# A four-layer graph network on one core: an addition moved one step in VectorE's order, and the first transposes of each attended pair laid apart

## The chip, the cores and the metric

The kernel runs on one core of a Trainium2 chip, in one launch. The metric is the time of one execution on the device in microseconds (us), as the median of several runs. A profile is one execution with every instruction recorded; its page and its views give times from the start of the span. The engines are named as the profile names them: PE is TensorE (matmuls and transposes), PEld its weight loads, DVE is VectorE, ACT is ScalarE, POOL is GpSimd, SP is the queue that issues the DMAs.

## The reference, cut to what matters

`x` has 3327 rows (nodes) of 256 numbers, `adj` is a 3327 x 3327 matrix, and all is fp32. Four layers follow one another, each `x = layernorm(x + layer(x, adj))`. The change lies in the fourth:

```python
def _top_p_attention(X, W1, W2, W3):
    logits = (X @ W1.T @ W2.T) @ (X @ W3.T).T
    probs = softmax(logits)
    ...                       # keep, in each row, the largest up to a sum of 0.9
    A = probs * mask
    return A / A.sum(-1)

R = (S + I) / rowsum          # S is adj
for n in range(2):
    A = _top_p_attention(Xa, W1, W2, W3)
    Xf = R @ Xf               # "diffusion"
    Xa = A @ Xa               # "attention"
    Z = Z + Xf @ U1[n].T + Xa @ U2[n].T
h = X + Z
```

The change touches the first of these two rounds only (n = 0), the "first attention".

## The kernel before, in words

The 3327 rows are padded to 26 tiles of 128 rows (`nt` = 26, `nh` = 13). In the first attention the tiles are worked in pairs, 13 of them. Each pair takes three kinds of work:

- Diffusion (`diffused_pair`, from L1219): R @ X for two row tiles at once, in 13 steps ("columns"). The seven products of a column are the seven of Strassen's scheme for a 2 x 2 block product (`products`, L1166); their operands are sums that VectorE makes (`cb`) from tiles that are loaded two columns at a time (`part`, L1221: three DMAs into `at`, three buffers).
- Attention (`attended_pair`, from L1250): the same seven products with the masked exponentials `es` of the pair. Here every column must first be transposed. `turn(j)` makes four transposes into one PSUM tile named `tp` and ScalarE copies it to `wt`; `mix()` makes the sums `sw` from `wt` in three VectorE instructions. Three columns are turned and two mixed ahead of the first product; from there each step turns column j + 3, mixes column j + 2 and multiplies column j.
- The two row tiles of the pair before are finished in `first` (from L1550), a generator of steps. It scales the attention's result on ScalarE, transposes it together with the diffused tile (`xt`, a VectorE copy out of a `tp` tile), multiplies by U1[0] and U2[0] into one half of a second `tp` tile, `ps`, and by U1[1] into its other half. VectorE adds X to the first half (`s`, stored in DRAM as `sd` over SP), ScalarE copies the second half into `Y`, which is the name of `F` in the profile. Another step makes the products with U2[1] (`pg`, a third `tp` tile) and the keys and queries of the second attention.

For a tile's exponentials there is a search for the top-p threshold, `search_short` (from L1388), a generator as well. Nearly all of it is VectorE's: 26 MAX8 over segments (`cand`), six rounds of MAX8 and MATCH_REPLACE (`top`, `rest`), a sum over the ranks (`lim`, `cs`, `over`, `v`), and two passes over the two halves of the tile `e`, each 1664 columns wide, that zero what falls below the threshold. ScalarE does the exponentials. A tile can be transposed only when the pass over its second half is done.

The order is written out by hand. During this part of the program PE and VectorE run strictly in the order in which the generators are stepped (the flag `fixed` and the class `Fixed`, L873 to L885). ScalarE, GpSimd and SP instructions are put in order by the framework's scheduler, which also makes every wait. The loop over the pairs (from L1739) interleaves the steps. For pair i it first runs a "stage" of seven steps, k = 0 to 6 (`stage`, L1692). Each step k gives

1. one column of the diffusion of pair i + 1 (`spread`),
2. what `then` holds for k: at k = 0 `end_pair` closes the attention of pair i - 1; at k = 5 `attend_to` finishes all open searches (`finish`), and takes the first step of pair i's attention,
3. on even k one group of logits of the next tile (four matmuls into `sc`, ScalarE copies them to `e`),
4. on k = 2, 3, 4 one step of `first`,
5. some steps of the running search (`looks`).

Seven attention columns follow, then a second stage of six steps with the rest of the diffusion, another tile's logits and `first` of the other tile of the pair before, and the last six attention columns. The pool `psum` gives `tp` two buffers, so that every new `tp` tile waits until the tile but one before has been read. The buffer `s` has one copy, which `first` uses twice: for the sum with X and later for the products with U2[1].

The lines that matter below: L1263 (ACT's copy `wt` in `turn`), L1404 and L1408 (ACT's exponentials in the search), L1160 and L1163 (ACT's copies of the logits), L1553, L1570 and L1577 (ACT in `first`), L1569 (the DMA of `s`), L1329 (ACT's copy in the last two tiles' attention, which are done one at a time). PE and VectorE instructions of this part all carry L891, the line of the helper that records the order.

Of the kernel before, what the change touches and what calls it, by code (L numbers as in the profile page):

```python
# [50 lines left out]
def gnn_kernel(ctx: ExitStack, tc: tile.TileContext, n: int, a: dict, out: bass.AP):  # L51
    nc = tc.nc
# [124 lines left out]
    with tc.tile_pool(name="l1b", bufs=1) as wpool, tc.tile_pool(name="l1at", bufs=2) as l1at:  # L177
# [3 lines left out]
        with tc.tile_pool(name="l0", bufs=1) as pool, tc.tile_pool(name="l0w", bufs=2) as work, \  # L181
# [30 lines left out]
            for i in range(nh):  # L212
# [12 lines left out]
                for r in range(2):  # L225
                    it = 2 * i + r
# [13 lines left out]
        with tc.tile_pool(name="l1aw", bufs=1) as cwork, tc.tile_pool(name="l1c", bufs=2) as ch, \  # L240
# [499 lines left out]
            turned = []  # L740
            for k, (c, s) in enumerate(states):
# [61 lines left out]
                if c and 9 <= s < 9 + tiles_of(c - 1):  # L803
                    rs, nb = plus[:2]
                    i = s - 9
# [44 lines left out]
            for i in range(m):  # L850
                it = starts[nch - 1] // P + i
# [16 lines left out]
    with tc.tile_pool(name="l3", bufs=1) as pool, tc.tile_pool(name="l3d", bufs=1, space=DRAM) as dram:  # L868
# [26 lines left out]
        def project_keys(ps, it, xt):  # L895

            h = it * P // half
            for k in range(2):
                tensor.matmul(ps, wkq[h][:, k, :], xt[:, k, :], start=(k == 0), stop=(k == 1))

        def store_keys(work, ps, p, it):

            h, j = divmod(it * P, half)
            key, query = (slice(x * DA, (x + 1) * DA) for x in (h, 1 - h))
            nc.scalar.copy(kT[p][key, j:j + P], ps[key, :])
            q = work.tile([2 * DA, P], F32, name="q")
            nc.scalar.copy(q[query, :], ps[query, :])
            for x in (0, DA):
                nc.sync.dma_start(qd[p][it, x:x + DA, :], q[query, :])
# [94 lines left out]
        with tc.tile_pool(name="l2c", bufs=1) as cpool:  # L1004
# [5 lines left out]
            with tc.tile_pool(name="l2a", bufs=1) as wpool, \  # L1010
# [36 lines left out]
                ps = psum.tile([1, 1], F32, name="ps")  # L1047
# [84 lines left out]
        Y = F[:, :, :D]  # L1132
# [33 lines left out]
        def products(pa, y, w, b):  # L1166

            own, mix = pa[:, 0, :], pa[:, 1, :]
            a11, a12, s1, a22, s2, s3, s4 = w
            b11, b21, b22, t1, t2, t3, t4 = b  # L1170
            for k, (acc, x, v) in enumerate(((own[:, :HD], a11, b11), (own[:, HD:D], a12, b21), (own[:, D:D + HD], s1, t1),
                                             (mix[:, :HD], s4, b22), (mix[:, HD:D], a22, t4),
                                             (mix[:, D:D + HD], s2, t2), (mix[:, D + HD:], s3, t3))):
                tensor.matmul(acc, x, v[:, y, :], start=(y == 0 and k in (0, 3)), stop=(y == nh - 1 and k in (2, 6)))

        def assembled(work, pa):

            p1, p2, p5, p3, p4, p6, p7 = (pa[:, k // 3, k % 3 * HD:(k % 3 + 1) * HD] if k < 6 else pa[:, 1, 3 * HD:] for k in range(7))
            c = work.tile([P, 2, D], F32, name="c", bufs=1)
            v, u = c[:, 0, HD:], c[:, 1, HD:]  # L1180
            vector.tensor_copy(v, p1)
            vector.tensor_add(c[:, 0, :HD], p2, v)
            vector.tensor_sub(v, p6, v)
            vector.tensor_sub(u, v, p7)
            vector.tensor_add(v, v, p5)
            vector.tensor_sub(v, p3, v)
            vector.tensor_sub(c[:, 1, :HD], u, p4)
            vector.tensor_add(u, u, p5)
            return c
# [62 lines left out]
        def attended_pair(quads, psum, es, b):  # L1252

            pa = psum.tile([P, 2, 512], F32, name="acc")
            wts, ws = [], []

            def turn(j):
                pt = psum.tile([P, 4, P], F32, name="tp")
                for r, e in enumerate(es):
                    for h in range(2):  # L1260
                        tensor.transpose(pt[:, 2 * r + h, :], e[:, (h * nh + j) * P:(h * nh + j + 1) * P], ident)
                wts.append(quads.tile([P, 4, P], F32, name="wt", bufs=4))
                nc.scalar.copy(wts[-1], pt)  # L1263

            def mix():
                wt = wts.pop(0)
                sw = quads.tile([P, 4, P], F32, name="sw", bufs=3)
                vector.tensor_tensor(sw[:, :2, :], wt[:, ::3, :], wt[:, 2:3, :].to_broadcast([P, 2, P]), op=ALU.add)
                vector.tensor_add(sw[:, 2, :], sw[:, 1, :], wt[:, 0, :])
                vector.tensor_add(sw[:, 3, :], sw[:, 2, :], wt[:, 1, :])  # L1270
                a11, a12, a21, a22, s3, s1, s2, s4 = (x[:, k, :] for x in (wt, sw) for k in range(4))
                ws.append((a11, a12, s1, a22, s2, s3, s4))

            for j in range(3):
                turn(j)
            for j in range(2):
                mix()
            yield None
            for j in range(nh):
                if j + 3 < nh:  # L1280
                    turn(j + 3)
                if wts:
                    mix()
                products(pa, j, ws.pop(0), b)
                yield None
            yield assembled(quads, pa)
# [263 lines left out]
        def first(work, psum, it, acc, f, xf, tag="pj", xa=None):  # L1550

            xa = work.tile([P, D], F32, name="h") if xa is None else xa
            nc.scalar.mul(xa, acc, f)  # L1553
            yield
            pt = psum.tile([P, 4, P], F32, name=tag)
            for i, v in enumerate((xf, xa)):
                for k in range(2):
                    tensor.transpose(pt[:, 2 * i + k, :], v[:, k * P:(k + 1) * P], ident)
            xt = work.tile([P, 4, P], F32, name="xt", bufs=1)
            vector.tensor_copy(xt, pt)  # L1560
            yield
            ps = psum.tile([P, 4, P], F32, name=tag).rearrange("p (k x) d -> p k (x d)", k=2)
            for k in range(4):
                tensor.matmul(ps[:, 0, :], xt[:, k, :], (u1 if k < 2 else u2)[:, 0, k % 2, :], start=(k == 0), stop=(k == 3))
            for k in range(2):
                tensor.matmul(ps[:, 1, :], xt[:, k, :], u1[:, 1, k, :], start=(k == 0), stop=(k == 1))
            s = work.tile([P, D], F32, name="s")
            vector.tensor_add(s, ps[:, 0, :], X[:, it, :])
            nc.sync.dma_start(sd[it], s)  # L1569
            nc.scalar.copy(Y[:, it, :], ps[:, 1, :])  # L1570
            yield
            pg = psum.tile([P, 4, P], F32, name=tag).rearrange("p (k x) d -> p k (x d)", k=2)
            for k in range(2):
                tensor.matmul(pg[:, 0, :], xt[:, 2 + k, :], u2[:, 1, k, :], start=(k == 0), stop=(k == 1))
            project_keys(pg[:, 1, :P], it, xt[:, 2:, :])
            g = G[:, it, :] if tag == "pj" else work.tile([P, D], F32, name="s")
            nc.scalar.copy(g, pg[:, 0, :])  # L1577
            if tag != "pj":
                nc.sync.dma_start(gd[it], g)
            store_keys(work, pg[:, 1, :P], 1, it)  # L1580
            yield
# [70 lines left out]
        with tc.tile_pool(name="l3w", bufs=2) as work, tc.tile_pool(name="l3s", bufs=4) as sm:  # L1652
# [13 lines left out]
            with tc.tile_pool(name="l3p", bufs=2, space=PSUM) as psum, tc.tile_pool(name="l3a", bufs=1) as quads:  # L1666
# [39 lines left out]
                def attend_to(i):  # L1706
                    turned[0] = attended_pair(quads, psum, (es[2 * i], es[2 * i + 1]), b)
                    finish()
                    next(turned[0])

                turned = [None]
                none = [iter(())]
                todo = [none, none]

                def end_pair(i):
                    c = next(turned[0])
                    for r in range(2):
                        it = 2 * i + r
                        f = normalizer(sm, kepts[0][:, it:it + 1], tots[0][:, it:it + 1])
                        todo[r] = [first(quads, psum, it, c[:, r, :], f, xfs[it], "tp", c[:, r, :])]  # L1720
                        next(todo[r][0])
                    ends[0] = todo[0][0]
# [15 lines left out]
                ends = [iter(())]  # L1738
                for i in range(nh - 1):  # L1739
                    stage(spread, 7, logits(2 * i + 2), ends, counts,  # L1740
                          {0: lambda: end_pair(i - 1) if i else None, 5: lambda: attend_to(i)})
                    counts = [1, 2, 2, 2, 2, 0, 0]
                    queue.append(searches[2 * i + 2])
                    values = turned[0]
                    for k in range(7):
                        next(values)
                        looks(k in (1, 2, 4, 5, 6))
                    stage(spread, 6, logits(2 * i + 3), todo[1], [2, 1, 2, 1, 2, 1], {})
                    finish()
                    queue.append(searches[2 * i + 3])  # L1750
                    for k in range(6):
                        next(values)
                        if k == 0:
                            for _ in spread:
                                pass
                        if k == 3:
                            spread = spreading(i + 2)
                        looks(k > 1)
# [245 lines left out]
```

## Time and profile before

| | us |
|---|---|
| median of 3 runs (3407.56, 3408.01, 3412.42) | 3408.01 |
| the profiled execution | 3412.8 |
| its span, first to last instruction | 3411.0 |
| PE busy in the span | 3129.6 (92%) |
| DVE busy | 2687.8 (79%) |
| ACT busy | 1729.9 (51%) |
| POOL busy | 1132.1 (33%) |

The profiled execution is 4.8 us above the median; 1.8 us of it lie outside the span. The first attention with its attended pairs lies between about 1755 and 2570 us of the span. Its 12 pairs of the loop repeat every 65.30 us: the fourth transpose of an attended pair starts at 1820.10, 1950.71, 2016.01, 2342.52 and 2473.13, for example, which are multiples of 65.30 apart. Busy time of PE is summed from modelled ends, and matmuls are pipelined; so the distance between the starts of two instructions is the surer measure of what a stretch takes. "[1.06 <-DVE e L891]" after an entry of the timeline means that the engine stood idle for 1.06 us before it and that a VectorE instruction on the tile `e` ended that wait. A count such as x5 joins five instructions of one kind into one entry, which begins with the first of them.

### The profile page before, as it was taken

The numbers are of one execution on the slowest core, as the hardware profiler recorded it, in microseconds if no ns is written. First come the engines' busy times: TensorE is split into PE (matmuls) and PEld (weight loads), VectorE is DVE, ScalarE is ACT, GpSimd is POOL, SyncE is SP. The second block draws the span as 40 slices with busy tenths as digits, with TensorE's granted clock in tenths as the row PEclk, the third lists the DMA queues.
The fourth block names the chain that finished last, engine by engine and source line by source line (L and its number), as shares of the span: only waits on it lengthen the run. The fifth ranks groups of instructions, "written<-read, shape, count | busy, mean of one in ns | idle before, by whom it ended". The sixth has DMA issues, their size and how long they took to land. (4 is left out here: it accounts for less than half of the span.)

```text
span 3411.0 us, 50267 instructions
## 1 busy us (share of the span) xinstructions
PE 3129.6 (92%) x18301; PEld 2561.4 (75%) x18301; DVE 2687.8 (79%) x5899; ACT 1729.9 (51%) x2763; POOL 1132.1 (33%) x1328
## 2 busy tenths in 40 slices
PE   8999888988888766999989999999997899999997
PEld 5999656666676555888868888888885677777776
DVE  4665268999999997877578778878863889999996
ACT  1000556767667676111133333333336888888883
POOL 0000145656665654111310000000003566666663
PEclk9999998999999888999989999999998999999999
DMA  6775334434343221544322222323213122222221
GB/s 198 249 254 190 111 99 118 113 109 113 102 122 90 67 59 42 177 139 152 111 88 79 81 72 80 87 65 88 79 49 108 40 68 67 64 63 73 72 63 36
DMA packets 206263, 344.31 MB, mean 101 GB/s; under 512 B 22222, under 2 KB 129166, under 8 KB 205870
## 3 DMA queue, kind: packets, MB, share of 16 engines
q1 hardware_dynamic: 205998, 340.92, 33.8%
q8 instruction: 148, 2.42, 0.3%
q14 instruction: 117, 0.96, 0.1%
HBM read 304.65 MB, written 36.21 MB: 100 GB/s over the span
## 5 line engine op out<-in xcount | busy, mean ns | idle before, releaser
L330 POOL TENSOR_TENSOR h<-du,row 128x2048 f32<-128x2048 f32 (+1 forms) x110 | 465.9, 4236 | 344.6 <-DVE hc L330 249.8
L330 DVE TENSOR_TENSOR_SCAN h<-dA,carry,h 128x512 f32<-128x512 f32 (+1 forms) x384 | 448.9, 1220 | 18.2 <-ACT dA L337 18.1
L337 ACT ACTIVATE dA<-t,A_log 128x512 f32<-128x512 f32 (+1 forms) x448 | 292.6, 658 | 146.9 <-DVE h L330 145.2
L1296 PE MATMUL acc<-F,at 128*128 128x256 f32 x1352 | 343.9, 383 | 3.0 <-DMA at<-in_adjT 2.1
L1341 PE MATMUL acc<-G,wt 128*128 128x256 f32 x1352 | 333.0, 388 | 6.6 <-ACT wt L1139 6.3
L1079 PE MATMUL acc<-F,at 128*128 128x257 f32 x1352 | 303.4, 381 | 0.7 <-ACT r L1023 0.7
L389 PE MATMUL cb<-F,at 128*128 128x256 f32 x1196 | 294.7, 394 | 8.3 <-ACT hn L409 3.4
L1341 PEld LDWEIGHTS acc<-G,wt 128*128 128x128 f32 x1352 | 249.1, 191 | 62.6 <-ACT wt L1139 32.7
L1146 POOL MEMSET e<- 128x1 f32 x52 | 4.9, 99 | 835.2 <-PE tp L891 770.1
L1296 PEld LDWEIGHTS acc<-F,at 128*128 128x128 f32 x1352 | 240.7, 190 | 53.2 <-issue 21.5
L1079 PEld LDWEIGHTS acc<-F,at 128*128 128x128 f32 x1352 | 253.4, 190 | 36.3 <-issue 1.0
L680 PE MATMUL y<-ident,hc 128*128 128x128 f32 x1664 | 235.5, 295 | 46.9 <-DVE hc L330 46.8
L680 PEld LDWEIGHTS y<-ident,hc 128*128 128x128 f32 x1664 | 209.2, 153 | 88.8 <-DVE hc L330 63.9
L389 PEld LDWEIGHTS cb<-F,at 128*128 128x128 f32 x1196 | 229.4, 198 | 58.5 <-issue 19.6
L330 DVE TENSOR_TENSOR hc<-h,row 128x2048 f32<-128x2048 f32 (+2 forms) x114 | 242.9, 2133 | 11.4 <-PE y L680 4.3
L891 PE MATMUL acc<-X,at 128*128 128x128 f32 (+1 forms) x988 | 173.7, 287 | 6.1 <-issue 6.1
L1263 ACT COPY wt<-tp 128x512 f32<-128x512 f32 x156 | 90.8, 589 | 166.1 <-PE tp L891 152.8
L138 PE MATMUL acc<-t,cb 128*128 128x128 f32 (+1 forms) x1014 | 168.4, 275 | 0.0
L891 PEld LDWEIGHTS acc<-X,at 128*128 128x128 f32 x988 | 142.2, 193 | 30.2 <-issue 25.3
L891 PE MATMUL acc<-G,sw 128*128 128x128 f32 x936 | 155.5, 275 | 0.0
L891 DVE MAX8 cand<-e 128x8 f32<-128x128 f32 x676 | 139.8, 277 | 5.5 <-ACT e L1160 3.8
L1160 ACT COPY e<-sc 128x832 f32<-128x832 f32 x78 | 65.9, 845 | 149.4 <-PE sc L891 149.4
(417 smaller groups left out, 7274.2 us busy)
## 6 DMA issues: line engine op xcount, KB each, us to landing
at<-in_adjT SPq DMA_DIRECT2D x54, 832.0 KB, 4.5
at<-in_adjT SPq DMA_DIRECT2D x130, 320.0 KB, 3.0
row<-bc SPq DMA_DIRECT2D x80, 512.0 KB, 5.1
at<-in_adjT SPq DMA_DIRECT2D x52, 640.0 KB, 5.5
at<-in_adjT SPq DMA_DIRECT2D x52, 576.0 KB, 4.3
at<-in_adjT SPq DMA_DIRECT2D x72, 256.0 KB, 3.2
at<-mixed SPq DMA_DIRECT2D x72, 256.0 KB, 3.6
mixed<-cb SPq DMA_DIRECT2D x26, 640.0 KB, 4.2
```

The costliest lines, as they stand in the source:

```text
L138: mm = nc.tensor.matmul(acc, w[:, j, :], x, start=(y == 0 and k % 3 == 0 and k < 6), stop=(y == nh - 1 and k in (2, 6)))
L330: return lambda *x, **k: tc.keep_in_program_order(op(*x, **k))
L337: decays.append(op(*x, **k))
L389: ten.matmul(acc, at[:, j % JC, :], X0[:, j, :], start=(j == 0), stop=(j == nt - 1))
L680: x = ten.matmul(y[:, g * P:(g + 1) * P], h[:, g, i * P:(i + 1) * P], ident, is_transpose=True, start=(first and g == 0), stop=(last and g ...
L891: return lambda *x, **k: tc.keep_in_program_order(op(*x, **k))
L1079: nc.tensor.matmul(acc, at[:, j, :], F[:, j0 + j, :], start=(j0 + j == 0), stop=(j0 + j == nt - 1))
L1146: nc.gpsimd.memset(e[:, n:], NEG)
L1160: copy(halves[:, :, c0:c0 + ws[0]], pl[:, :, :ws[0]])
L1263: nc.scalar.copy(wts[-1], pt)
L1296: nc.tensor.matmul(acc, at[:, j, :], rhs[:, j0 + j, :], start=(j0 + j == 0), stop=(j0 + j == nt - 1))
L1341: tensor.matmul(acc, wt[:, j, :], rhs[:, j0 + j, :], start=(j0 + j == 0), stop=(j0 + j == nt - 1))
```

## The change

Two edits. In `first` the VectorE addition of X and the DMA of its result stand behind the `yield`, thus in the next step; ScalarE's copy of the other half of the same PSUM tile now comes ahead of them. In `attended_pair` the preparation of three columns, one step before, is three steps: column 0 is turned at k = 5 as before; column 1 is turned and column 0 mixed at k = 6, after the diffusion's column of that step; column 2 is turned and column 1 mixed after the stage, when the logits of k = 6 have been issued. `go_on` takes those steps. No instruction is added or left out.

```diff
-            for j in range(3):
-                turn(j)
-            for j in range(2):
-                mix()
+            turn(0)
+            yield None
+            turn(1)
+            mix()
+            yield None
+            turn(2)
+            mix()
             yield None
             for j in range(nh):
                 if j + 3 < nh:
...
             for k in range(2):
                 tensor.matmul(ps[:, 1, :], xt[:, k, :], u1[:, 1, k, :], start=(k == 0), stop=(k == 1))
+            nc.scalar.copy(Y[:, it, :], ps[:, 1, :])
+            yield
             s = work.tile([P, D], F32, name="s")
             vector.tensor_add(s, ps[:, 0, :], X[:, it, :])
             nc.sync.dma_start(sd[it], s)
-            nc.scalar.copy(Y[:, it, :], ps[:, 1, :])
-            yield
             pg = psum.tile([P, 4, P], F32, name=tag).rearrange("p (k x) d -> p k (x d)", k=2)
...
+                def go_on():
+                    next(turned[0])
+
...
                     stage(spread, 7, logits(2 * i + 2), ends, counts,
-                          {0: lambda: end_pair(i - 1) if i else None, 5: lambda: attend_to(i)})
+                          {0: lambda: end_pair(i - 1) if i else None, 5: lambda: attend_to(i), 6: go_on})
+                    go_on()
                     counts = [1, 2, 2, 2, 2, 0, 0]
```

## The prediction

> **What bounds the kernel now.** The page's 40 slices came first. Both edits lie in the first attention, where PE is busy at 9 tenths and its clock is at 9 tenths or full. I then asked for the busy time of each engine over single pairs of that part (columns: length, then busy time and count of PE, PEld, DVE, ACT, POOL, then the granted clock).
>
> ```profile
> 1883.80:1949.10 65.30, 64.00 (x499) 56.96 (x498) 52.12 (x177) 24.18 (x39) 0.20 (x2) 1.00 0.28 79
> 1949.10:2014.40 65.30, 64.00 (x499) 56.96 (x498) 52.18 (x177) 24.18 (x39) 0.20 (x2) 1.00 0.27 79
> ```
>
> The reader is to see that PE works 64.00 of 65.30 us, at full clock, and that DVE has some 13 us to spare: PE is the bound, and all that an order of work can win here is its idle time, nominally 1.30 us a pair. The waits over the whole part, 1750 to 2570 us (total, times, longest), say where that is:
>
> ```profile
> ACT F L1570 <- DVE s L891: 79.2, 23, 4.7
> ...
> PE tp L891 <- DVE e L891: 21.9, 13, 9.0
> ...
> PE tp L891 <- ACT wt L1263: 2.6, 11, 0.2
> ```
>
> PE waits before transposes of `e`, for DVE's search and for the copy that frees a `tp` tile. The 13 waits of 21.9 us are 8.96 and 1.33 us in the first pair, where the searches have no lead yet, and 1.06 in each of the other eleven. The timeline of PE around one of these (start, length, what):
>
> ```profile
> 1891.52 0.60 PE L891 MATMUL tp<-ident,e 128*128 128x128 f32 x4
> 1891.95 0.61 PE L891 MATMUL acc<-X,wt 128*128 128x128 f32 x4
> ...
> 1941.04 2.75 PE L891 MATMUL tp<-U,xt 128*128 128x256 f32 x12
> ...
> 1949.16 0.49 PE L891 MATMUL tp<-ident,e 128*128 128x128 f32 x3
> 1950.71 0.76 PE L891 MATMUL tp<-ident,e 128*128 128x128 f32 x5 [1.06 <-DVE e L891]
> 1951.72 0.66 PE L891 MATMUL tp<-ident,e 128*128 128x128 f32 x4 [0.24 <-ACT wt L1263]
> 1952.21 0.61 PE L891 MATMUL acc<-X,at 128*128 128x128 f32 x4
> ...
> 1953.87 0.97 PE L891 MATMUL sc<-kT,q 64*128 64x416 f32 x4
> 1954.76 0.66 PE L891 MATMUL tp<-ident,e 128*128 128x128 f32 x4
> 1955.26 0.61 PE L891 MATMUL acc<-X,wt 128*128 128x128 f32 x4
> ```
>
> Undisturbed, four transposes take 0.43 us from start to start (1891.52 to 1891.95), 0.11 each. At 1949.16 three go, and the fourth, the second half of the odd tile, waits. Why DVE is late is in its own timeline:
>
> ```profile
> 1941.65 0.36 DVE L891 MATCH_REPLACE8 rest<-top,rest 128x208 f32<-128x208 f32 x1
> 1943.84 0.42 DVE L891 TENSOR_TENSOR s<-tp,X 128x256 f32<-128x256 f32 x1 [1.82 <-PE tp L891]
> 1944.18 0.37 DVE L891 MAX8 top<-rest 128x8 f32<-128x208 f32 x1
> ...
> 1945.35 0.67 DVE L891 TENSOR_TENSOR cb<-at 128x512 f32<-128x512 f32 x1
> 1945.94 0.15 DVE L891 TENSOR_SCALAR lim<-tot 128x1 f32<-128x1 f32 x1
> ...
> 1948.70 1.95 DVE L891 SCALAR_TENSOR_TENSOR e<-e,v 128x1664 f32<-128x1664 f32 x1
> 1950.58 0.08 DVE L891 DVE_READ_ACCUMULATOR e<-e,v 128x1 f32 x1
> ```
>
> DVE has nothing left from 1942.02 and stands 1.82 us at the addition of X, until PE's U products end (1941.04 + 2.75 = 1943.79). Two ranks of the search, ready to run, are queued behind it, and from there DVE is busy without a gap until the tile is ready. The addition's idle time is thus the cause of PE's. Last, ACT:
>
> ```profile
> 1944.30 0.37 ACT L1570 COPY F<-tp 128x256 f32<-128x256 f32 x1 [2.40 <-DVE s L891]
> ...
> 1946.31 0.85 ACT L1160 COPY e<-sc 128x832 f32<-128x832 f32 x1 [0.51 <-PE sc L891]
> ```
>
> ACT's copy of the other half of the same PSUM tile starts only when DVE's addition has ended (1943.84 + 0.42 = 1944.26), though it needs nothing of it.
>
> [...] 23 waits of ACT `F` for DVE `s`. So the changed order turns this wait round: DVE's addition will wait for ACT's copy. [...]
>
> **Part 1, the addition a step later.** It removes DVE's wait at k = 3. DVE runs the last two ranks from about 1942.04 (1941.65 + 0.36, and a start), 1.17 us by the old rows (1944.18 to 1945.35), to 1943.21. At k = 4 `cb` follows, 0.59 from start to start (1945.35 to 1945.94), to 1943.80. It needs its loads: SP issued that part at 1936.40 to 1938.17 in this pair, and the median to landing is 3.6 us, so about 1941.8; no wait. Then the addition. ACT's copy can start when DVE's addition did, 1943.84, lasts 0.37, and hands on with 0.04 to 0.05 (1944.26 to 1944.30 above): the addition starts at 1944.26, and `lim` 0.34 later (1943.84 to 1944.18), at 1944.60 instead of 1945.94. The top ranks' exponential on ACT (L1408, 0.33 us) has its data from 1943.3 and fits before or behind the copy. From `lim` to the end of the last accumulator read is 1950.66 - 1945.94 = 4.72 us, so the tile is ready at 1949.32, and the fourth transpose could start at 1949.37 with the 0.05 us it takes now. PE comes to it at 1949.16 + 3 x 0.11 = 1949.49. The wait goes, with 0.12 us to spare. By starts that is 1950.71 - 1949.49 = **1.22 us a pair**; more than the 1.06 listed, since listed idle time begins at a modelled end.
>
> Queued behind the addition are `lim` and the two passes, that is PE's tile, so a late copy on ACT is the danger; it is rival 3. The DMA of `s` moves with it by 0.4 us (1944.29 to about 1944.7), past nothing on SP: the loads of the next part are issued by 1943.6 and the next instruction there is at 1948.20. The copy of `pg` reuses the buffer `s` at 1947.80 and needs that DMA landed; 1944.7 + 2.0 (median to landing) = 1946.7, hidden by 1.1 us. In the second stage of six steps the same move lets one rank run in a 1.50 us wait of DVE at 1915.15, and delays the addition by the same 0.4; no PE work waits there, so I cost it at nothing. For the last tile nothing covers it: ACT's copy of `pg` at 2569.65 waits for that DMA, the queries of the second attention come behind it, and PE's first logits there wait 1.93 us for them. Adding the copy's 0.37 and the handover costs **0.4 us once**.
>
> **Part 2, the transposes apart.** Now turn 1 follows turn 0 at once and turn 2 needs the `tp` buffer of turn 0: it starts at 1951.72 instead of 1950.71 + 5 x 0.11 = 1951.26, **0.46 us a pair**. With a column of the diffusion (1.57 us, as an attended one from 1889.95 to 1891.52) and four logit matmuls (0.89) between the turns, each copy has over 1.3 us where 0.65 is needed. New order from 1949.16: turn 0 0.43, column 1.57, turn 1 0.48, logits 0.90, turn 2 0.50, turn 3 0.43, first product at 1953.47 instead of 1955.26. This check gives 1.79 us where the two waits give 1.68; I take the smaller. The sums for the first product (`mix` 0) start when the `wt` copy of turn 0 is there, about 1950.4, and end 1.04 later, two us ahead of need. DVE's `cb` of k = 6 now comes ahead of `mix` 0; its loads were issued by 1943.6.
>
> **The sum.** 11 pairs x (1.22 + 0.46) = 18.5; the first pair nothing, for its waits are the searches' own lateness; the end + 0.4. So - 18.1 us on the profiled execution's 3412.8, 3394.7. That execution is 4.8 above the median 3408.0; from the median, **3390**. Bounds of the unknown costs: if the copies hand over 0.3 us slower, the 0.12 us of spare and 0.2 a pair go, 2 us; if the check is the better figure, 1.2 us more. With some 2 us of scatter between runs, 3385 to 3395 for this case.
>
> **Rivals.**
> 1. The search still ends last: part 1 brings nothing, because another item (`cb`'s loads, the exponential on ACT) holds DVE back until 1945.94. Against it: no idle time before `cb` or `lim` there. Left: 11 x 0.46 - 0.4 = 4.7, 3403.
> 2. The scheduler puts ACT's `wt` copy of turn 1 behind the copy of the logits (L1163, 0.91 us for both halves). It would start at 1953.5, end at 1954.1 and hold turn 3, due at 1953.0, by 1.15 us: 18.1 - 12.7 = 5.4, 3403. Against it: turn 1 is ahead of the logits in PE's order.
> 3. Slower: ACT's `F` copy lands behind the logits copy of k = 4, which waits for PE until 1946.31. Then the copy runs at 1947.10 to 1947.47, the addition at 1947.51, `lim` at 1947.85, the tile is ready at 1952.57, and PE's fourth transpose comes 1.92 later than now. Less the 0.46 of part 2: + 1.46 x 11 + 0.4 = 16.5, 3424.5. It decides from an addition later than 1946.06, 1.8 us behind my figure. For it: ACT's order isn't written by hand, and the addition now hangs on it. Against it: the copy's data are there 2.4 us before those logits.
>
> **How the numbers follow.** Forecast 0.80, rival 1 0.07, rival 2 0.04, rival 3 0.07, 0.02 for anything else. About 0.2%, 6.8 us, is what a measurement can tell from no change. Faster by more: the forecast and a share of rival 2, 0.83; within it rivals 1 and most of 2, 0.09; slower 0.08. The range, 3385 to 3402, holds the forecast and the faster ends of rivals 1 and 2.
>
> **What would show it.** Right: a pair's period of 63.6 us, PE idle near nothing in it; PE's waits for DVE `e` down from 21.9 to about 10.3 us in 2 cases, those for ACT `wt` gone; ACT `F` no longer waiting for DVE `s`, but DVE `s` some 0.4 us for ACT `F`. Wrong: waits of DVE `s` for ACT above 1 us, or of turn 3 for a `wt` copy. A period still over 65 would leave part 1 as empty.

## The result, and the profile after

The changed kernel takes 3392.5 us in the median of six runs (3390.88 to 3397.72); the kernel before took 3410.52 in six runs beside it (3407.56 to 3418.32). The ratio is 0.995, with a 95% interval from 0.994 to 0.996: 18.0 us less by the medians. The profiled execution took 3392.58, its span is 3390.8 instead of 3411.0. The 20.2 us between the two spans divide so, by the starts of the same instructions in both traces:

| stretch | before | after | difference |
|---|---|---|---|
| start to the fourth transpose of the first pair | 1757.23 | 1753.10 | -4.1 |
| "the section": from there to VectorE's cast of `fi`, which closes the first attention | 811.8 | 792.7 | -19.2 |
| from the cast to PE's first logits of the second attention | 1.59 | 1.95 | +0.4 |
| from there to the cast that closes the second attention | 827.06 | 829.79 | +2.7 |

The 13.3 us behind the last row are the same in both. The first and the last row hold no instruction that the change touches, and they move against each other; they are scatter between executions (the changed kernel, run again as `e10_changed_again`, has 1751.10 and 828.3 there). What the change did is in the two rows between, -18.8. The periods tell it more sharply: busy time by engine over two pairs of the changed kernel, with the columns that the prediction explained.

```profile
1877.93:1941.49 63.56, 63.56 (x498) 56.94 (x497) 52.45 (x177) 24.16 (x39) 0.20 (x2) 1.00 0.28 81
1941.49:2005.05 63.56, 63.56 (x498) 56.94 (x497) 52.45 (x177) 24.16 (x39) 0.20 (x2) 1.00 0.27 81
```

A pair takes 63.56 us instead of 65.30, and the profile shows PE busy in all of it, at full clock. Another order has next to nothing left to win in these pairs; less work for PE would shorten them. The waits from 1750 to 2570 us:

```profile
DVE s L891 <- ACT F L1570: 29.3, 24, 4.5
...
ACT F L1570 <- PE tp L891: 23.2, 26, 4.2
...
PE tp L891 <- DVE e L891: 10.1, 2, 8.7
```

The wait of ACT's copy for DVE's addition is gone and has turned round: the addition now waits for the copy. PE's waits before transposes of `e` are the two of the first pair (8.73 and 1.33 us), and its waits for the copy `wt` are no longer in the list. The timeline of PE around a first turn:

```profile
1933.37 2.76 PE L891 MATMUL tp<-U,xt 128*128 128x256 f32 x12
...
1941.49 0.60 PE L891 MATMUL tp<-ident,e 128*128 128x128 f32 x4
1941.93 0.61 PE L891 MATMUL acc<-X,at 128*128 128x128 f32 x4
...
1943.49 0.60 PE L891 MATMUL tp<-ident,e 128*128 128x128 f32 x4
1944.02 0.97 PE L891 MATMUL sc<-kT,q 64*128 64x416 f32 x4
1944.92 1.09 PE L891 MATMUL tp<-ident,e 128*128 128x128 f32 x8
1945.85 0.61 PE L891 MATMUL acc<-X,wt 128*128 128x128 f32 x4
```

All four transposes of turn 0 go in one row, a column of the diffusion stands ahead of turn 1, and the logits ahead of turns 2 and 3. From turn 0 to the first product it is 1945.85 - 1941.49 = 4.36 us; it was 6.10. VectorE and ScalarE ahead of it:

```profile
1907.88 0.42 DVE L891 TENSOR_TENSOR s<-tp,X 128x256 f32<-128x256 f32 x1 [1.61 <-ACT F L1570]
...
1935.26 0.38 DVE L891 MAX8 top<-rest 128x8 f32<-128x208 f32 x1
1935.56 0.67 DVE L891 TENSOR_TENSOR cb<-at 128x512 f32<-128x512 f32 x1
1936.57 0.42 DVE L891 TENSOR_TENSOR s<-tp,X 128x256 f32<-128x256 f32 x1 [0.34 <-ACT F L1570]
1936.91 0.14 DVE L891 TENSOR_SCALAR lim<-tot 128x1 f32<-128x1 f32 x1
...
1941.55 0.08 DVE L891 DVE_READ_ACCUMULATOR e<-e,v 128x1 f32 x1
```

```profile
1936.17 0.37 ACT L1570 COPY F<-tp 128x256 f32<-128x256 f32 x1 [0.16 <-PE tp L891]
1938.64 0.85 ACT L1160 COPY e<-sc 128x832 f32<-128x832 f32 x1 [2.10 <-PE sc L891]
```

The U products end at 1933.37 + 2.76 = 1936.13. ACT copies 0.04 later; DVE, which has meanwhile finished its ranks and `cb`, waits 0.34 us and not 1.82. The tile is ready at 1941.63, and PE's fourth transpose is due at 1941.49 + 3 x 0.11 = 1941.82. In the second stage (1907.88) DVE waits 1.61 us for the copy, where it waited 1.50 for PE before; no wait of PE follows from it.

### The profile page after: what moved, and what is told of

Its sections match the earlier page's. It is cut to its first block, busy times and chain, and to the rows that moved or that the text cites. A ratio compares the mean times of both kernels' runs of the same rounds, so it can differ in the third digit from the quotient of the medians.

```text
span 3390.8 us, 50286 instructions
## 1 busy us (share of the span) xinstructions
PE 3121.1 (92%) x18301; PEld 2560.0 (75%) x18301; DVE 2692.5 (79%) x5899; ACT 1730.8 (51%) x2763; POOL 1133.6 (33%) x1328
```

## The experiments

Each ratio is against the kernel before, run beside it. Five questions: are the two parts separate and additive; what does an early copy do without the later addition; what would a late copy (the slower rival) have cost; how much was spare; and is anything left to win?

### One part at a time

`e1_add_only` is the changed kernel with the three turns at one step again:

```diff
-            turn(0)
-            yield None
-            turn(1)
-            mix()
-            yield None
-            turn(2)
-            mix()
+            for j in range(3):
+                turn(j)
+            for j in range(2):
+                mix()
...
-                          {..., 5: lambda: attend_to(i), 6: go_on})
-                    go_on()
+                          {..., 5: lambda: attend_to(i)})
```

> The addition of X one step later alone; the three turns stay together. Theory (two separate waits, each edit removes its own): the odd tile is ready 1.2 to 1.3 us earlier, so PE's wait before the fourth transpose of a pair goes (1.06 us listed, 1.22 by starts), while turn 2 still waits some 0.4 us for the tp buffer. A pair's period 65.30 - 1.22 = 64.1 us; in all 11 x 1.22 - 0.4 at the end = 13 us under the kernel before, ratio 0.996. Rival (the packed turns are the cause, the search is not): the period stays within 0.3 us of 65.30 and the ratio within 0.001 of 1.

`e2_turns_only` keeps the turns apart and has `first` as it was:

```diff
-            nc.scalar.copy(Y[:, it, :], ps[:, 1, :])
-            yield
             s = work.tile([P, D], F32, name="s")
             vector.tensor_add(s, ps[:, 0, :], X[:, it, :])
             nc.sync.dma_start(sd[it], s)
+            nc.scalar.copy(Y[:, it, :], ps[:, 1, :])
+            yield
```

> The turns laid apart alone; the addition of X stays in its old step. Theory: the fourth transpose waits 1.06 us for the tile as before, since turn 0 still stands ahead of the diffusion's column; only the 0.46 us of turn 2 go. Period 64.8 us, in all 5 to 6 us under the kernel before, ratio 0.9984. Rival (the packed turns are the main cause): period 64 us or less, 14 us or more under the kernel before, ratio 0.996 or less.

Measured: `e1_add_only` 0.9964 [0.9951, 0.9977], a period of 64.02 us, the section 798.1 (-13.7). `e2_turns_only` 0.9991 [0.9982, 1.0], a period of 64.85, the section 806.5 (-5.3). PE's timeline at a first turn, of the addition alone and then of the turns alone:

```profile
1817.42 1.04 PE L891 MATMUL tp<-ident,e 128*128 128x128 f32 x8
1818.70 0.66 PE L891 MATMUL tp<-ident,e 128*128 128x128 f32 x4 [0.24 <-ACT wt L1263]
```

```profile
1814.16 0.49 PE L891 MATMUL tp<-ident,e 128*128 128x128 f32 x3
1815.71 0.33 PE L891 MATMUL tp<-ident,e 128*128 128x128 f32 x1 [1.06 <-DVE e L891]
1815.88 0.61 PE L891 MATMUL acc<-X,at 128*128 128x128 f32 x4
```

Each removes its own wait and leaves the other's as it was: eight transposes in a row and 0.24 us for the `wt` copy in the first, the fourth transpose 1.06 us late in the second. Their gains in the section add up to 19.0 us, where the whole change has 19.2. (The medians give 10.9 and 2.8 us, with intervals of some 4 us to either side for the first and 3 for the second; the section of the profile is the sharper measure.) So they are two separate waits, one behind the other on PE, and neither hid the other.

### The copy early, the addition where it was

`e3_copy_first` is the kernel before, with ACT's copy ahead of the addition in the same step. It has the first half of what the edit in `first` does, and not the `yield`:

```diff
+            nc.scalar.copy(Y[:, it, :], ps[:, 1, :])
             s = work.tile([P, D], F32, name="s")
             vector.tensor_add(s, ps[:, 0, :], X[:, it, :])
             nc.sync.dma_start(sd[it], s)
-            nc.scalar.copy(Y[:, it, :], ps[:, 1, :])
             yield
```

> The kernel before with one thing changed: ACT's copy of the other half of the PSUM tile is traced ahead of DVE's addition, both in the old step. Theory (the two reads of one PSUM tile are kept apart, in the order in which they are traced): DVE's addition now waits for ACT's copy, 0.42 us later than before; the tile is ready 0.42 later and PE's wait before the fourth transpose grows from 1.06 to about 1.48. Period 65.7 us, in all 11 x 0.42 + 0.4 = 5 us over the kernel before, ratio 1.0015. Rival (ACT merely came later by its queue's order): the addition starts with the end of PE's products as before, period 65.30, ratio 1.000 within 0.001.

Measured: 1.0036 [1.0024, 1.0047], the section 824.3 (+12.5, where 5 were expected). DVE's timeline:

```profile
1877.43 0.42 DVE L891 TENSOR_TENSOR s<-tp,X 128x256 f32<-128x256 f32 x1 [1.89 <-ACT F L1567]
```

The mechanism is as expected: DVE waits for the copy and not for PE, the search is 0.4 us later, and PE's wait for the tile grows from 1.06 to 1.46. (DVE's idle time here is only 0.07 above the 1.82 of before, since DVE comes to the addition later as well.) But that explains only 11 x 0.41 = 4.5 us. The periods show where the rest is: six of the ten are 65.71 us, 0.41 above the 65.30 of before, but four are 67.3, 1.6 us more. PE's timeline in a slow pair, and in the next:

```profile
1950.01 0.77 PE L891 MATMUL tp<-ident,e 128*128 128x128 f32 x5 [1.46 <-DVE e L891]
...
1951.78 1.06 PE L891 MATMUL acc<-X,at 128*128 128x128 f32 x4
...
1954.80 0.97 PE L891 MATMUL sc<-kT,q 64*128 64x416 f32 x4
...
2017.35 0.77 PE L891 MATMUL tp<-ident,e 128*128 128x128 f32 x5 [1.46 <-DVE e L891]
...
2018.85 0.61 PE L891 MATMUL acc<-X,at 128*128 128x128 f32 x4
...
2020.50 0.97 PE L891 MATMUL sc<-kT,q 64*128 64x416 f32 x4
```

The wait is the same 1.46 us, but the column behind it takes 1954.80 - 1951.78 = 3.02 us in one and 1.65 in the other. The windows of the two (columns as before; the clock is the third number from the right):

```profile
1951.00:1954.40 3.40, 3.38 (x17) 3.39 (x18) 3.20 (x10) 1.04 (x2) 0.00 (x0) 0.53 0.50 149
...
2017.30:2020.70 3.40, 3.11 (x25) 2.76 (x27) 2.39 (x8) 1.67 (x3) 0.00 (x0) 1.00 0.69 193
```

In the slow pair the granted clock is 0.53 over 3.4 us. This happens in five of the eleven pairs (0.53 to 0.58 in the same window of each, 1.00 in the other six; the fifth is the last pair, which no period follows), and 5 x 1.6 = 8 with the 4.5 makes the 12.5 us. In the kernel before, with its wait of 1.06 us, the granted clock is 1.00 from 1762.0 to 2570.9 us. Why the same wait costs clock in one pair and not in the next was not shown.

### The slower rival, built

Rival 3 had the copy `F` land behind the copy of the logits of k = 4. First attempt, `e4_late_copy`: the copy stands behind the `yield`, and ACT is held to the written order for it and for the logits' copies.

```diff
-            copy = in_order(nc.scalar.copy) if p else nc.scalar.copy
+            copy = in_order(nc.scalar.copy) if p or fixed else nc.scalar.copy
...
-            nc.scalar.copy(Y[:, it, :], ps[:, 1, :])
             yield
+            in_order(nc.scalar.copy)(Y[:, it, :], ps[:, 1, :])
             s = work.tile([P, D], F32, name="s")
```

> The changed kernel with ACT's copy F put behind ACT's copy of the logits of step k = 4 (the order of rival 3 of the prediction). Theory (the search hangs on that copy): the addition starts about 3.2 us later than in the changed kernel, PE's fourth transpose of a pair waits some 3 us; period 65.30 + 1.46 = 66.8 us, 11 x 1.46 + 0.4 = 16.5 us over the kernel before, ratio 1.005. Rival (DVE has enough lead to hide it): period under 64.5 us, as the changed kernel's 63.57 within 1 us.

Measured: 1.0154 [1.0136, 1.0172], about three times what was expected. Its waits also include 12.5 us of PE for ACT's logits (`sc`, 10 times), so the second edit did something of its own. `e5_late_copy2` holds only the copy `F` behind the logits of k = 4, in both stages of a pair, and leaves the others to the scheduler. (`in_order` is a helper at L1139, so that the profile gives this line to the copy.)

> Only the copy F is put behind ACT's logits copy of step k = 4; all other copies keep the order of the changed kernel. The search's two transposes then wait about 3.1 us by starts in a pair, against none in the changed kernel and 1.22 in the kernel before. Theory (an idle PE also loses clock: the run with the copy first showed 1.6 us more in every second pair, at a wait of 1.46): period 66.7 us where the clock holds, 1.6 us more in half of the pairs or in all; in all 25 to 34 us over the kernel before, ratio 1.0075 to 1.010. Rival (the clock has no part; the surplus of the earlier run with late copies came from the other copies' order): 66.7 us in every pair, 16.5 us over, ratio 1.005.

Measured: 1.0148 [1.0134, 1.0161], thus 52 us over by the medians (49.8 in the section) where 25 to 34 were expected. So most of the excess is not the logits' order. The waits of `e5_late_copy2` from 1740 to 2600 us, then its timelines in the second and in the first stage, of DVE and, for the first stage, of ACT:

```profile
DVE s L891 <- ACT F L1139: 93.8, 24, 5.7
...
PE tp L891 <- DVE e L891: 39.8, 24, 8.7
...
PE tp L891 <- DVE xt L891: 9.7, 10, 1.0
...
PE acc L891 <- DVE sw L891: 6.3, 22, 0.4
```

```profile
1920.74 0.42 DVE L891 TENSOR_TENSOR s<-tp,X 128x256 f32<-128x256 f32 x1 [4.83 <-ACT F L1139]
...
1951.76 0.42 DVE L891 TENSOR_TENSOR s<-tp,X 128x256 f32<-128x256 f32 x1 [3.05 <-ACT F L1139]
```

```profile
1950.60 0.85 ACT L1160 COPY e<-sc 128x832 f32<-128x832 f32 x1 [2.11 <-PE sc L891]
1951.35 0.38 ACT L1139 COPY F<-tp 128x256 f32<-128x256 f32 x1
```

The copy runs straight behind the logits' copy, as rival 3 had it. DVE loses 4.83 us in the second stage, and from there to the first stage's addition it is busy without a gap; PE meets its lateness at `xt` (0.97 us a pair) and `sw` (0.41 and 0.16). Six of ten periods are 69.05, the other four 70.65, again 1.6 apart. To separate the second stage, `e9_late_even` has the late copy in the even tiles alone, which are those of the first stage:

```diff
-            nc.scalar.copy(Y[:, it, :], ps[:, 1, :])
-            yield
+            late = fixed and it % 2 == 0
+            if not late:
+                nc.scalar.copy(Y[:, it, :], ps[:, 1, :])
+            yield
+            if late:
+                tc.keep_in_program_order(nc.scalar.copy(Y[:, it, :], ps[:, 1, :]))
             s = work.tile([P, D], F32, name="s")
             vector.tensor_add(s, ps[:, 0, :], X[:, it, :])
```

> The late copy F only in the first stage of a pair (the even tiles); in the second stage it comes first, as in the changed kernel. Theory (rival 3 of the prediction was undersized because the late copy of the second stage also makes VectorE late, and because the waits cost clock): PE's waits for xt and sw, 0.96 and 0.6 us a pair with the copy late in both stages, go; left are 3.1 us before the turns; period 66.7 us where the clock holds and 68.3 where it is halved for one 3.4 us stretch; in all 20 to 30 us over the kernel before, ratio 1.006 to 1.009. Rival (the second stage has no part): 52 us over as with both, ratio 1.015.

Measured: 1.0098 [1.0084, 1.0113], 36 us over by the medians and 30.7 in the section, a little more than expected. The waits of a pair at `xt` and `sw` are gone, and each pair has 1.16 us at the third transpose and 1.54 at the fourth:

```profile
1956.71 0.33 PE L891 MATMUL tp<-ident,e 128*128 128x128 f32 x1 [1.16 <-DVE e L891]
1958.58 0.47 PE L891 MATMUL tp<-ident,e 128*128 128x128 f32 x1 [1.54 <-DVE e L891]
```

A pair at full clock repeats in 66.71 us, nearly 65.30 + 1.46, the rival's own sum; but only the first does, the others take 68.16 to 68.27. Windows over the end of the waits and what follows, in a pair that lost clock and in one that did not:

```profile
1958.50:1961.90 3.40, 3.32 (x16) 3.32 (x17) 1.89 (x7) 0.59 (x1) 0.00 (x0) 0.52 0.42 128
1823.70:1827.10 3.40, 3.38 (x25) 2.62 (x26) 2.20 (x6) 1.28 (x3) 0.00 (x0) 1.00 0.39 122
```

The first line is the pair that lost it: 16 matmuls in 3.40 us instead of 25, at half the clock. So a late copy has three prices: its own lateness in the first stage, 1.4 us a pair; the second stage's, 69.05 - 66.71 = 2.3; and the clock, 1.5 to 1.6 in the pairs that lose it (11 x 1.41 + 10 x 1.5 = 30.5; the section grew by 30.7).

### How much was spare

The changed kernel with two more MAX8 in the search, whose results nothing uses, ahead of the two passes:

```diff
             yield
+            spare = sm.tile([P, 8], F32, name="spare")
+            for _ in range(2):
+                vector.max(spare, cand)
             sums = t1(sm, "sums", 2)
```

> The changed kernel with two more MAX8 (about 0.4 us each, result unused) in each search ahead of its two passes. Theory (the tile is ready just in time, with some 0.14 us to spare): the tile comes 0.75 to 0.8 us later, PE waits 0.6 us by starts in each of the eleven pairs, period 64.2 us, 7 us over the changed kernel, ratio to the kernel before 0.9966[...]. Rival (VectorE has slack to hide it): period 63.57 as in the changed kernel, ratio 0.995.

Measured: 0.9967 [0.9955, 0.9979], a period of 64.05. Lines of DVE's timeline and of PE's:

```profile
1935.48 0.78 DVE L891 MAX8 spare<-cand 128x8 f32<-128x208 f32 x2
```

```profile
1939.30 0.49 PE L891 MATMUL tp<-ident,e 128*128 128x128 f32 x3
1940.06 0.33 PE L891 MATMUL tp<-ident,e 128*128 128x128 f32 x1 [0.27 <-DVE e L891]
```

The wait of the fourth transpose is back. The tile is 0.55 us later (5.27 us from `lim` to its end instead of 4.72; 0.75 to 0.8 were expected). The fourth transpose, due at 1939.30 + 3 x 0.11 = 1939.63, starts 0.43 late, so 0.55 - 0.43 = 0.12 us was spare. The period is 0.48 longer (63.57 by starts in the changed kernel), because a wait costs PE a little behind it too: from this transpose to the next matmul it is 0.16 us (1940.06 to 1940.22), where transposes in a row are 0.11 apart. Behind the wait of 0.27 us no pair is longer than another: the ten periods are 64.04 to 64.06 us.

### What is left

Two waits of the changed kernel were tried. `e7_fill_first` fills the 8.73 and 1.33 us of the first pair with five columns of the next diffusion and three groups of logits, ahead of its first turn (`fill`). The steps of the running search are laid otherwise for it in that pair, and its second stage takes what is left of those logits:

```diff
                     turned[0] = attended_pair(quads, psum, (es[2 * i], es[2 * i + 1]), b)
+                    if i == 0:
+                        fill(2)
+                        looks(3)
+                        fill(2)
                     finish()
+                    if i == 0:
+                        fill(1)
                     next(turned[0])
```

> The changed kernel with the first pair's wait filled: five columns of its diffusion and three of the four logit groups of tile 3, which came in the second stage of that pair, are put ahead of its first turn, and some steps of tile 1's search behind two of VectorE's column sums. Theory (PE is the bound everywhere else, so work moved into the wait of 8.7 + 1.3 us is won): the tile is 1.3 us later for two column sums, some 10 us of PE work go into the wait and the clock stays up; VectorE, 51 us busy in that pair, then bounds it, which leaves 5 to 8 us: ratio to the kernel before 0.993. Rival (the next pair's tile is late by as much as was won): ratio 0.995 as in the changed kernel, with PE waiting 5 us or more in the second pair.

Measured: 0.9945 [0.9933, 0.9956], not to be told from the changed kernel. The two waits are gone; there is one of 1.66 us for `cb` in the filled part instead, and a long one later in the same pair. Its PE and then its DVE timeline there:

```profile
1791.33 0.80 PE L891 MATMUL acc<-G,sw 128*128 128x128 f32 x2 [6.41 <-DVE sw L891]
```

```profile
1788.79 1.95 DVE L891 SCALAR_TENSOR_TENSOR e<-e,v 128x1664 f32<-128x1664 f32 x1
...
1790.86 0.42 DVE L891 TENSOR_TENSOR sw<-wt 128x256 f32<-128x256 f32 x1
```

The sums `sw` stand in DVE's order behind the search of the next tile, whose last pass ends at 1790.74, and the columns of the diffusion that ran beside that search in the changed kernel have been spent. Was it DVE's total work? `e11_fill_gpsimd` gives the sums `cb` of two diffusions to GpSimd, where one takes 1.27 us instead of 0.68:

```diff
-                vector.tensor_tensor(cb[:, :, :m, :], ...)
+                (nc.gpsimd if i in (1, 2) else vector).tensor_tensor(cb[:, :, :m, :], ...)
```

> The filled first pair and the earlier keys together, and the column sums cb of the second and third pair's diffusion on GpSimd, which is idle in this part, in place of VectorE. Theory (VectorE bounded the first pair: it took 6.4 us back from PE in that pair's later columns): VectorE is spared 9 x 0.6 = 5.4 us there, the tile isn't delayed by sums, and the wait of 6.4 us falls to under 2: 5 to 8 us under the changed kernel, ratio to the kernel before 0.993. Rival (GpSimd's sums, over 1 us each, hold PE, or the later tile is late all the same): ratio 0.9945 or more.

Measured: 0.9947 [0.9935, 0.9959], and the wait for `sw` is 6.41 us again. So that theory falls: what holds the sums is what is queued ahead of them in that stretch, and no `cb` is among it. (This kernel has the next one's edit as well.)

`e8_keys_first` puts, for the last tile alone, the keys and queries ahead of ACT's copy of `pg`, the one that waits for the DMA of `s`:

```diff
+            if it == nt - 1 and fixed:
+                store_keys(work, pg[:, 1, :P], 1, it)
-            nc.scalar.copy(g, pg[:, 0, :])
+            (in_order(nc.scalar.copy) if it == nt - 1 and fixed else nc.scalar.copy)(g, pg[:, 0, :])
...
-            store_keys(work, pg[:, 1, :P], 1, it)
+            if it < nt - 1 or not fixed:
+                store_keys(work, pg[:, 1, :P], 1, it)
```

> The changed kernel with ACT's copies of the last tile's keys and queries ahead of its copy of the products with U2[1], which waits for the DMA of s. Theory (PE's 2.28 us of waiting for the queries at the start of the second attention hang on that DMA through ACT's order): the wait falls to under 0.7 us, 1.5 to 2 us in all, ratio to the kernel before 0.9945. Rival: the wait is only replaced by one for the copies of the first logits, ratio 0.995.

Measured: 0.9941 [0.9929, 0.9953]. PE's timeline at the second attention's first logits:

```profile
2545.83 0.97 PE L1154 MATMUL sc<-kT,q 64*128 64x416 f32 x4 [1.63 <-ACT s L1139]
```

The wait is 1.63 us, 2.28 in the changed kernel, not under 0.7 as expected, and its last releaser is now the copy itself. That is 0.65 us in the profile and, in the times, nothing that can be told apart from the changed kernel, of which one more set of runs gave this:

> The changed kernel itself, as the measure beside the next one: ratio to the kernel before 0.995, PE without waits from the second pair to the twelfth.

Measured: 0.9945 [0.9932, 0.9958], median 3391.04, its second attention 828.3 us.

## Why the prediction held, point by point

- **The sum.** Forecast 11 x (1.22 + 0.46) less 0.4, 18.1 us, and 3390 us. Measured: 1.74 a pair by the period and +0.4 at the end, 18.8 in the profile and 18.0 by the medians. The predicted time started from the three runs shown, whose median was 3408.01; beside the changed kernel the kernel before had 3410.52.
- **Part 1, 1.22 us.** The addition alone gave 65.30 - 64.02 = 1.28. The steps hold as well: from the end of the U products to `lim` 0.81 us forecast and 0.78 measured (1936.91 - 1936.13), to the ready tile 5.53 and 5.50. The 1.06 us listed as idle was too small a figure, and the distance of starts nearly the right one. What it lacks is the restart: behind the wait, the transpose hands on after 0.164 us instead of 0.109 (1815.71 to 1815.88 in `e2_turns_only`), 0.055 more, which brings 1.22 to 1.28.
- **Part 2, 0.46 us.** The turns alone gave 65.30 - 64.85 = 0.45. The figure is right, its working is so by luck. Five transposes behind the wait take 0.60 us in the trace and not 5 x 0.11, so that turn 2 was due at 1951.31 and waited 0.40 by starts, not 0.46; the restart behind its own wait is the other 0.055.
- **Which of the two sums.** The waits gave 1.68 a pair, the check of the new order 1.79. Measured are 1.74: two waits of 1.22 and 0.40 and a restart of 0.055 behind each, of which the sum held only one. The check took 4.31 us from turn 0 to the first product, and it is 4.36.
- **Spare, 0.12 us.** The timeline after gives 1941.82 - 1941.63 - 0.05 = 0.14, and `e6_search_longer` 0.12. The change stands that close to a new wait.
- **First pair at nothing.** From the fourth transpose to the first product it took 6.41 us before and 6.34 after, and both long waits stayed.
- **Second stage at nothing.** True here, though DVE waits 1.61 us there. The sign that the prediction named, "waits of DVE `s` for ACT above 1 us", was therefore too coarse: what counts is what is queued behind the wait, and in the first stage that is PE's next tile. It is also true only while the copy is early: with a late copy the second stage cost 2.3 us a pair.
- **The end, 0.4 us once.** PE's wait there went from 1.93 to 2.28, and the stretch grew by 0.36.
- **Rivals 1 and 2** didn't come: no item held DVE back, and ACT copied `wt` of turn 1 in time, as no wait of PE for it shows.
- **Rival 3** didn't come either: the copy ran 0.04 us after its data, 2.5 us ahead of the logits' copy. Its mechanism is real and its first-stage term was right (66.71 - 65.30 = 1.41, forecast 1.46), but its price was mis-sized: 16.5 us forecast, 36 by the medians with the copy late in the first stage alone (`e9_late_even`), 52 with both (`e5_late_copy2`). It left out the clock and the second stage. The danger was two to three times what the prediction weighed.
- **The shared PSUM tile.** Its two readers were kept apart in each order: ACT's copy waited 23 times for the addition before (79.2 us in all), and the addition 24 times for the copy after (29.3 us). `e3_copy_first` shows that which of them waits is set by the order in which the program names them (there the addition waits 1.89 us for the copy), and that turning it round without the `yield` costs 0.41 us a pair.

What stays open: the logits' order of `e4_late_copy` was not run without the late copy. Beside it, it hardly counts: the shorter periods are 69.13 us there and 69.05 in `e5_late_copy2`. Nor is it known whether another order in the first pair, with the sums moved ahead of the search, would gain.

## What to carry to other kernels

Where an engine that runs in order stands at an instruction whose data come from elsewhere, look at what is ready behind it and who waits for that; moving the instruction one step later is worth the distance to the next thing that comes due, here 1.28 us, and not the whole stall of 1.82. Before such a move, see who else reads the same PSUM tile and in which order, since here that decided which engine waited for the other (ACT 23 times before, DVE 24 times after). Count a wait by the distance of starts, add what the restart behind it costs (here 0.055 us), and don't fill one hole with the work that covers the next.

## What the runs showed of the hardware

In these runs a short wait sometimes cost PE more than its length. In `e3_copy_first`, after waits of 1.46 us (with 0.24 us more one microsecond later), the granted clock was 0.53 to 0.58 over 3.4 us in five of the eleven pairs, and 1.00 in the other six. In `e9_late_even`, after 1.16 and 1.54 us close together, the first pair ran on at 1.00; in the other ten the fourth transpose took 0.47 to 0.48 us where it takes 0.33 in the first, and the one of them in the windows above had a clock of 0.52. In `e5_late_copy2` the two waits are the same, and five of the eleven pairs were slowed: from the third transpose to the next logits PE took 4.95 to 5.64 us there, and 4.13 in the other six. A pair of each kind, in the 3.4 us that begin 3.4 us behind the third transpose (columns as before):

```profile
1818.70:1822.10 3.40, 3.40 (x28) 2.64 (x27) 1.73 (x6) 2.24 (x5) 0.00 (x0) 1.00 0.11 33
...
1887.75:1891.15 3.40, 3.40 (x14) 2.08 (x14) 1.30 (x5) 0.62 (x2) 0.00 (x0) 0.56 0.04 11
```

By the periods, a slowed pair is 1.5 to 1.6 us longer in all three runs. After 1.06 us with the same 0.24, in the kernel before, the clock was 1.00 in every pair, and after 0.27 us, in `e6_search_longer`, no period stands out.

What decides between two pairs with the same waits was not shown. In `e3_copy_first` the slowed ones are every second pair, with the fourth transpose at 1950.01, 2083.06, 2216.11, 2349.12 and 2482.13 us, and PE waited 1.46 or 1.47 us in all eleven. So the clock's part in the price of a late copy is a figure of these runs and can't be carried over to another wait.
